# Cross-attention with LayerNorm: the order of the last stores, of the last products and of one tile's scaling

## The chip, the cores and the metric

The kernel runs on one core of one Trainium2 chip. The metric is the device time of one execution in microseconds (us). Times of the kernel before come from three runs and from one execution taken by the hardware profiler.

## What is computed

For each of 4 sequences, 2048 rows of 512 values attend to 77 context rows, with 16 heads of 32 columns. The result goes through an output projection, the input is added, and each row is normalised.

```
qs = x @ wq;  ks = ctx @ wk;  vs = ctx @ wv           # split in 16 heads of 32
scores = qs @ ks.T / sqrt(32);  scores[mask] = -inf
attn = softmax(scores) @ vs                            # heads joined again: 512 columns
out = attn @ wo + x
mu, var = mean(out), mean((out - mu)**2)               # over the 512 columns of a row
return (out - mu) / sqrt(var + 1e-5) * gamma + beta
```

## The kernel before

The 8192 rows are 64 tiles of 128 rows, two tiles to a block; tile 63 is the last. The order in which work is recorded is written out by hand: ORDER is a string of words, each a letter for a step and the number of a tile or block, and a loop runs through it. Each engine takes its instructions in this order and waits for others by semaphores. Buffers and PSUM banks are handed out by another table, SLOTS.

The words that matter here, for tile t:

- `Wt` is the product of the attention weights with the values (`av_tile`, TensorE). Before it, `U` words issue DMAs that regroup the transposed weights, each on the queue that its last letter names (s SyncE, a ScalarE, g GpSimd). `ct` and `dt` write the high part AH (ScalarE) and the low part AL (VectorE, L540) of that product.
- `Ot` is the output projection (`o_proj`, L579): for each of 4 chunks of 128 rows three products, AH with the high weights, AH with the low weights, AL with the high weights, all summed in one PSUM bank `po`. Some numbers in PADS put idle steps ahead of products.
- `+t`, `@t`, `$t`, `=t`, `st`, `ut` add the input and work out mean and inverse root: `$` adds into PSUM (VectorE, L591), `s` takes the statistics on VectorE (L630, L632), `=` takes them on ScalarE instead (L636, L637; tiles 60 and 62), `u` is the inverse root on GpSimd, two small operations (L645 or L643, then L646), and `@` is `u` and one step more.
- Two ways lead from there to the result. On one, `%t` scales and shifts on ScalarE (L654), and `ft` multiplies by gamma and adds beta on GpSimd (`affine`, L621 and L622). On the other, `yt` centres and multiplies by gamma on VectorE (L659), and `zt` multiplies by the inverse root and adds beta on VectorE (`finish`, L662). Tiles 52, 55, 58 and 61 end in `f`; tiles 54, 56, 57, 59, 60 and 62 end in `z`. Tile 63 ends in two halves, `>63.0` and `>63.1` (L666).
- `wt` stores the tile, always on SyncE's queue (`store`, L625). Tile 63's halves go out as `<63.0` on SyncE and `<63.1` on ScalarE (L672).

Rows of tiles 56 to 59 lie in a buffer called xth and those of tiles 60 to 63 in one called xtl; those before in buffers called o.

Of the kernel before, what the change touches and what calls it, by code (L numbers as in the profile page):

```python
# [13 lines left out]
ALU = mybir.AluOpType  # L14
# [15 lines left out]
NC_D = D // P  # L30
# [12 lines left out]
KSCALE = 1.0 / HD**0.5  # L43
LATE = 48
LAST = 56

# [89 lines left out]
m63.1 P30.7a b29.1 O58 %55 u57 t62 %53 f55 %52 $56 U62.2s U62.11a V30 $54 U62.1s U62.10a +58 U62.6s U62.3a f53 t63  # L138
U62.4a O59 a30.0 a30.1 s58 U63.4s U63.1a U63.11s b30.0 @58 U62.8a U62.9s b30.1 U62.0a s56 U62.7s O61 U63.9a U62.5g
y57 U63.10g U63.3a s54 U63.6g U63.0s U63.5a U63.7g U63.2s y54 U63.8a u54 w50 O60 +61 %58 f52 w53 z54 s61 $59 y56  # L140
W62 @61 s59 W63 c62 u56 z57 u59 c63 d62 O62 $60 f58 y59 =60 d63 z59 %61 y60 O63 w59 u60 =62 z56 w58 f61 z60 w57 y62
w56 w60 s63 w52 w55 u62 y63 w61 u63 z62 w54 w62 >63.0 <63.0 >63.1 <63.1
"""

SLOTS = {
# [33 lines left out]
def xattn_layernorm(  # L179
# [15 lines left out]
    nc = tc.nc  # L195
# [12 lines left out]
    def buf(shape, dtype, tag, name):  # L208
        pool = tiny if shape[-1] <= H else sb
        return pool.tile(shape, dtype, tag=tag + next(slots[tag]), name=name)  # L210

    def once(held, key, shape, dtype, tag):
        if key not in held:
            held[key] = buf(shape, dtype, tag, f"{tag}_{key}")
        return held[key]

    def bank(name):
        return ps.tile([P, 512], F32, tag="mm" + next(slots["mm"]), name=name)
# [6 lines left out]
    woh = const.tile([P, NC_D, D], F32R, name="woh")  # L225
    wol = const.tile([P, NC_D, D], F32R, name="wol")
    kct = const.tile([P, NG, NB, NK2], F32, name="kct")
    vsb = const.tile([NK2, NB, 2, D // 2], F32, name="vsb")
    gam = const.tile([P, D], F32, name="gam")
    bet = const.tile([P, D], F32, name="bet")  # L230
# [28 lines left out]
    od, pos, mvs, rns, vd, ris, parts = {}, {}, {}, {}, {}, {}, {}  # L259
# [17 lines left out]
    def pad_steps():  # L277
        n = int(next(pads, "0"), 36)
        return [0] + [n // 11 + (i < n % 11) for i in range(11)]

    def idle(n):
        for _ in range(n):
            nc.tensor.nop(hint="pad")
# [259 lines left out]
    def load_x(t):  # L543
        if t < LAST:
            od[t] = buf([P, D], F32, "o", name=f"o_{t}")
        else:
            od[t] = once(ends, t // 4, [P, 4, D], F32, "xth" if t < LAST + 4 else "xtl")[:, t % 4]
        nc.sync.dma_start(od[t], x[t * P : (t + 1) * P, :])
# [19 lines left out]
    def o_proj(t):  # L568
        b, tt = divmod(t, 2)
        rs = slice(tt * P, tt * P + P)  # L570
        ah, al = ahs[b], als[b]
        first = t not in pos
        if first:
            pos[t] = bank(f"po_{t}")
        steps = pad_steps()
        for c in range(NC_D):
            for n, (a, w) in enumerate(((ah, woh), (ah, wol), (al, woh))):
                idle(steps[3 * c + n])
                nc.tensor.matmul(  # L579
                    pos[t],  # L580
                    a[:, c, rs],
                    w[:, c, :],
                    start=(first and c == 0 and n == 0),
                    stop=(c == NC_D - 1 and n == 2),
                )

    def residual(t):
        nc.vector.tensor_tensor(od[t], pos.pop(t), od[t], ALU.add)
# [16 lines left out]
    def rsqrt(b):  # L605
        rn = rns[b] = buf([P, 2, 2], F32, "rn", name=f"rn_{b}")
        mv = mvs[b]
        nc.gpsimd.tensor_tensor(rn[:, 0, :], mv[:, :, 1], eps, ALU.add)
        nc.gpsimd.tensor_tensor(rn[:, 0, :], rn[:, 0, :], mhalf, ALU.pow)
        nc.gpsimd.tensor_tensor(rn[:, 1, :], mv[:, :, 0], rn[:, 0, :], ALU.mult)  # L610
        nc.gpsimd.tensor_tensor(rn[:, 1, :], rn[:, 1, :], mneg, ALU.mult)

    def scale(t):
        o = od[t]
        tt = t % 2
        rn = rns[t // 2]
        nc.scalar.activation(o, o, AF.Identity, bias=rn[:, 1, tt : tt + 1], scale=rn[:, 0, tt : tt + 1])

    def affine(t):
        o = od[t]  # L620
        nc.gpsimd.tensor_tensor(o, o, gam, ALU.mult)  # L621
        nc.gpsimd.tensor_tensor(o, o, bet, ALU.add)  # L622

    def store(t):
        nc.sync.dma_start(out[t * P : (t + 1) * P, :], od.pop(t))  # L625
# [14 lines left out]
    def rsqrt_one(t):  # L640
        mv = mvs[t, 1]
        if t in by_act:
            nc.gpsimd.tensor_scalar(mv[:, 2:3], mv[:, 1:2], 1.0 / D, EPS, ALU.mult, ALU.add)  # L643
        else:
            nc.gpsimd.tensor_tensor(mv[:, 2:3], mv[:, 1:2], eps[:, :1], ALU.add)  # L645
        nc.gpsimd.tensor_tensor(mv[:, 2:3], mv[:, 2:3], mhalf[:, :1], ALU.pow)  # L646
# [9 lines left out]
    def centre(t):  # L656
        o = pos.get(t, od[t])
        m, op = (3, ALU.add) if t in by_act else (0, ALU.subtract)
        nc.vector.scalar_tensor_tensor(o, o, mvs[t, 1][:, m : m + 1], gam, op, ALU.mult)  # L659

    def finish(t):
        nc.vector.scalar_tensor_tensor(od[t], pos.pop(t, od[t]), mvs[t, 1][:, 2:3], bet, ALU.mult, ALU.add)  # L662
# [23 lines left out]
    first = [buf([P, 2, BLK + D], F32, tag, name=f"first_{tag}") for tag in ("xtl", "xth")]  # L686
    first = [first[c // 2][:, c % 2] for c in range(NC_D)]
# [21 lines left out]
    for c in range(NC_D):  # L709
# [12 lines left out]
        for n, (w, r) in enumerate(((wqh, x0h), (wqh, x0l), (wql, x0h))):  # L722
            for m in range(NG):
# [4 lines left out]
                    start=(c == 0 and n == 0),  # L728
                    stop=(c == NC_D - 1 and n == 2),
# [13 lines left out]
    for c in range(0, NC_D, 2):  # L743
# [19 lines left out]
        "V": lambda k, part: av(k), "W": lambda k, part: av_tile(k), "a": av_hi, "b": av_lo,  # L763
        "c": lambda k, part: av_hi(k // 2, k % 2, True), "d": lambda k, part: av_lo(k // 2, k % 2, True),
        "x": lambda k, part: load_x(k), "X": lambda k, part: resid(k), "O": lambda k, part: o_proj(k),
        "+": lambda k, part: residual(k), "s": lambda k, part: (moments_one if k >= LATE else moments)(k),
        "v": lambda k, part: rsqrt(k), "k": lambda k, part: scale(k), "f": lambda k, part: affine(k),
        "u": lambda k, part: rsqrt_one(k), "y": lambda k, part: centre(k), "z": lambda k, part: finish(k),
        "w": lambda k, part: store(k), "*": lambda k, part: hold(k), "#": lambda k, part: residual_late(k),
        "&": lambda k, part: split_hi(k, nc.scalar), "~": lambda k, part: split_lo(k),  # L770
# [63 lines left out]
```

## Time and profile before

| What | Value |
|---|---|
| Runs | 509.96, 510.60, 510.66 us; median 510.6 |
| Span of the profiled execution | 508.1 us, first to last instruction |
| Busy in that span | TensorE 98%, VectorE 93%, ScalarE 92%, GpSimd 83% |
| SyncE's last DMA issues | from 498.40 to 504.70 us |
| ScalarE's last DMA issue | 505.10 us |

The span is that of one profiled execution. The page gives no other time of that execution, and the time of a run is some 2 us longer than the span. Times inside the span are counted from its first instruction. A row of a timeline gives start, length, engine and line, then what is written and read. Matmuls overlap, so a row's length is more than the distance to the next one.

### The profile page before, as it was taken

To read this page: it belongs to the slowest core of one execution; us is meant where nothing else is said; L and a number is where in the kernel's file an instruction comes from. 1 tells how busy PE (TensorE), PEld (TensorE's weight loads), DVE (VectorE), ACT (ScalarE), POOL (GpSimd) and SP (SyncE) were. 2 spreads that over 40 slices of the span, in tenths; PEclk is the share of its full clock that TensorE was granted. 3 is DMA by queue.
4 is the path that set the end of the run, shared out by engine and by line. 5 is a ranking of instruction groups with operands and counts; after the bars stand their busy time and mean duration, and the time that the engine had idled before them with its cause. 6 is when DMAs were issued, how large, how long until landed. Compare 5 with 4: busy or idle time off the path is not lost.

```text
span 508.1 us, 21810 instructions
## 1 busy us (share of the span) xinstructions
PE 497.6 (98%) x6834; PEld 384.0 (76%) x6834; DVE 471.3 (93%) x2565; ACT 465.6 (92%) x2228; POOL 420.0 (83%) x388
## 2 busy tenths in 40 slices
PE   8999999999999999999999999999999999999994
PEld 6987777777777777777777877777787777776663
DVE  5798999999999999999999999999999999999986
ACT  6699999998999999999999999999999999999622
POOL 2573756999978998989899898888989679999986
PEclk9999999999999999999999999999999999999999
DMA  8947767878987687796877678777777687777755
GB/s 298 397 154 215 177 185 171 239 195 237 261 239 220 192 243 198 204 261 189 237 205 239 198 218 229 213 226 211 225 207 219 182 225 214 209 210 198 213 153 228
DMA packets 59236, 110.96 MB, mean 218 GB/s; under 512 B 9430, under 2 KB 12270, under 8 KB 59126
## 3 DMA queue, kind: packets, MB, share of 16 engines
q1 hardware_dynamic: 54854, 101.63, 69.1%
q0 software_dynamic: 2624, 6.16, 4.4%
q10 hardware_dynamic: 1648, 1.77, 1.4%
q8 instruction: 60, 0.98, 0.9%
q14 instruction: 50, 0.41, 0.3%
HBM read 41.79 MB, written 16.78 MB: 115 GB/s over the span
## 4 chain that ended last, share of the span: by engine, by line
PE 85%; DVE 5%; DMA 4%; POOL 3%; SPq 2%; issue 1%; ACTq 0%; ACT 0%; DVEq 0%
PE pq L290 33%; PE po L579 28%; PE sc L414 10%; PE pa L507 10%; PE pv L341 2%; DVE pbuf L431 1%; DVE B L482 1%; PE pk L313 1%; DMA xtl<-x 1%; DMA PT<-B 1%; SPq L493 1%; DMA first_xth<-xw 1%; POOL mvt L646 1%; PE pq L724 1%; DVE q L304 0%
## 5 line engine op out<-in xcount | busy, mean ns | idle before, releaser
L446 ACT ACTIVATE pbuf<-pbuf,nm 128x77 f32<-128x77 f32 x1024 | 352.4, 350 | 3.6 <-DVE nm L431 3.4
L446 ACT ACTIVATION_READ_ACCUMULATOR pbuf<-pbuf,nm 128x1 f32 x1024 | 195.3, 191 | 0.0
L431 DVE CUSTOM_DVE_ANT_0 pbuf<-sc,mb 128x77 f32<-128x77 f32 x1024 | 170.8, 232 | 6.8 <-PE sc L414 3.6
L461 POOL TENSOR_TENSOR pbuf<-pbuf,ri 128x1232 f32<-128x1232 f32 x63 | 142.8, 2268 | 29.1 <-DVE ri L456 27.6
L579 PE MATMUL po<-woh,AH 128*128 128x512 f32 x256 | 102.1, 399 | 0.4 <-DVE nm L431 0.4
L290 PE MATMUL pq<-xth,wqh 128*128 128x512 f32 (+1 forms) x256 | 101.2, 395 | 0.3
L579 PE MATMUL po<-woh,AL 128*128 128x512 f32 x256 | 99.8, 390 | 0.8 <-DVE AL L540 0.8
L579 PE MATMUL po<-wol,AH 128*128 128x512 f32 x256 | 99.7, 390 | 0.0
L290 PE MATMUL pq<-xth,wql 128*128 128x512 f32 (+1 forms) x256 | 98.1, 383 | 0.0
L290 PE MATMUL pq<-xtl,wqh 128*128 128x512 f32 (+1 forms) x256 | 98.1, 383 | 0.0
L482 DVE STREAM_TRANSPOSE B<-pbuf 128x1280 f32<-128x1280 f32 x64 | 96.1, 1501 | 0.9 <-POOL pbuf L461 0.2
L431 DVE DVE_READ_ACCUMULATOR2_ANT nm<- 128x1 f32 x1024 | 83.8, 82 | 0.0
L273 POOL TENSOR_TENSOR xtl<-xtf,xth 128x1024 fp32r<-128x1024 f32 x28 | 67.3, 2406 | 4.3 <-ACT xth L269 4.3
L622 POOL TENSOR_TENSOR o<-o,bet 128x512 f32<-128x512 f32 x51 | 66.0, 1294 | 4.0
L414 PEld LDWEIGHTS sc<-kct,q 32*64 32x64 f32 x4096 | 51.2, 130 | 22.2 <-issue 11.0
L621 POOL TENSOR_TENSOR o<-o,gam 128x512 f32<-128x512 f32 x51 | 67.0, 1314 | 0.2 <-issue 0.2
L414 PE MATMUL sc<-kct,q 32*64 32x77 f32 x4096 | 60.6, 238 | 0.0
L507 PE MATMUL pa<-PT,vsb 96*32 96x256 f32 x992 | 59.7, 382 | 0.0
L579 PEld LDWEIGHTS po<-woh,AH 128*128 128x128 f32 x256 | 48.0, 188 | 13.9 <-issue 1.7
L290 PEld LDWEIGHTS pq<-xth,wqh 128*128 128x128 f32 x256 | 48.1, 188 | 12.3 <-issue 1.2
L579 PEld LDWEIGHTS po<-woh,AL 128*128 128x128 f32 x256 | 48.1, 188 | 11.6 <-DVE AL L540 1.5
L290 PEld LDWEIGHTS pq<-xth,wql 128*128 128x128 f32 x256 | 48.1, 188 | 9.7
(127 smaller groups left out, 641.9 us busy)
## 6 DMA issues: line engine op xcount, KB each, us to landing
PT<-B SPq DMA_DIRECT2D x337, 128.0 KB
xtf<-xT SPq DMA_DIRECT2D x28, 512.0 KB
o<-x SPq DMA_DIRECT2D x56, 256.0 KB
out<-o SPq DMA_DIRECT2D x56, 256.0 KB
PT<-B POOLq DMA_DIRECT2D x29, 128.0 KB, 3.9
stage_a<-wk SPq DMA_DIRECT2D x4, 256.0 KB
stage_b<-wo SPq DMA_DIRECT2D x4, 256.0 KB
stage_a<-xT SPq DMA_DIRECT2D x2, 512.0 KB
```

The source lines that it names most:

```text
L273: nc.gpsimd.tensor_tensor(l[:, c : c + 2], fx.pop((g, c)), xh[g][:, c : c + 2].bitcast(F32), ALU.subtract)
L290: nc.tensor.matmul(pq, w[:, c, m * P : (m + 1) * P], r[g][:, c, rs], start=(n == 0), stop=(n == 11))
L341: nc.tensor.matmul(pv[: rows.stop - rows.start], ctx_s[c][i][:, rows], v[c], start=(n == 0), stop=(n == 11))
L414: mm = nc.tensor.matmul(sc[j][r0 : r0 + SR, g * NK : (g + 1) * NK], qs[q, g, rs.start + r0 : rs.start + r0 + SR], kct[q, g, t // TPB, keys ...
L431: nc.vector.tensor_tensor_reduce(pb[:, h // 2, (h % 2) * NK : (h % 2 + 1) * NK], scs[t][j][:, g * NK : (g + 1) * NK], mb[:, t % TPB, keys_ ...
L446: nc.scalar.activation(pb[:, h // 2, (h % 2) * NK : (h % 2 + 1) * NK], pb[:, h // 2, (h % 2) * NK : (h % 2 + 1) * NK], AF.Exp, bias=nmax[t ...
L461: nc.gpsimd.tensor_tensor(pv, pv, rv.to_broadcast((P, NP, 2, NK)), ALU.mult)
L482: nc.vector.transpose(bt.rearrange("p c q r -> p q c r"), pbuf[t % NPB].rearrange("p q (c r) -> p q c r", c=5),)
L507: nc.tensor.matmul(pas[b, g // 2][HD * j : HD * (j + 1), (g % 2) * BLK : (g % 2 + 1) * BLK], vsb[:, 2 * b // TPB, h % 2, HD * (h // 2) : H ...
L579: nc.tensor.matmul(pos[t], a[:, c, rs], w[:, c, :], start=(first and c == 0 and n == 0), stop=(c == NC_D - 1 and n == 2),)
L621: nc.gpsimd.tensor_tensor(o, o, gam, ALU.mult)
L622: nc.gpsimd.tensor_tensor(o, o, bet, ALU.add)
```

## The change

Three edits at the end of the program. The stores of tiles 55, 54, 52 and 57 are recorded before that of tile 59. The projections of tiles 62 and 63 take their eight products with AH first and the four with AL last. Tile 61's `f` is split in its two operations, written `|61.0` and `|61.1`: the multiplication now stands behind the inverse root of tile 62, the addition behind that of tile 63, and with that tile 62's `z` moves ahead of tile 63's statistics, and tile 61's store to the end.

```diff
+LOW_LAST = 62
...
-W62 @61 s59 W63 c62 u56 z57 u59 c63 d62 O62 $60 f58 y59 =60 d63 z59 %61 y60 O63 w59 u60 =62 z56 w58 f61 z60 w57 y62
-w56 w60 s63 w52 w55 u62 y63 w61 u63 z62 w54 w62 >63.0 <63.0 >63.1 <63.1
+W62 w55 w54 @61 s59 W63 c62 w52 u56 z57 u59 c63 d62 O62 $60 w57 f58 y59 =60 d63 z59 %61 y60 O63 w59 u60 =62 z56 w58
+z60 w56 u62 y62 w60 |61.0 z62 s63 w62 u63 y63 |61.1 >63.0 <63.0 >63.1 <63.1 w61
...
-        for c in range(NC_D):
-            for n, (a, w) in enumerate(((ah, woh), (ah, wol), (al, woh))):
-                idle(steps[3 * c + n])
...
+        terms = [(c, a, w) for c in range(NC_D) for a, w in ((ah, woh), (ah, wol), (al, woh))]
+        if t >= LOW_LAST:
+            terms.sort(key=lambda term: term[1] is al)
+        for i, (c, a, w) in enumerate(terms):
+            idle(steps[i])
+            nc.tensor.matmul(pos[t], a[:, c, rs], w[:, c, :], start=(first and i == 0), stop=(i == len(terms) - 1))
...
     def affine(t):
-        o = od[t]
-        nc.gpsimd.tensor_tensor(o, o, gam, ALU.mult)
-        nc.gpsimd.tensor_tensor(o, o, bet, ALU.add)
+        affine_step(t, 0)
+        affine_step(t, 1)
+
+    def affine_step(t, i):
+        nc.gpsimd.tensor_tensor(od[t], od[t], (gam, bet)[i], (ALU.mult, ALU.add)[i])
```

GpSimd (POOL), its last rows before. In a name the number after the letters is the tile; mvt holds a tile's statistics, gam and bet are gamma and beta, and xtl is here tile 61.

```order
L643 TENSOR_SCALAR mvt_60_10505<-mvt_60_10505 128x1
L646 TENSOR_TENSOR mvt_60_10505<-mvt_60_10505,small_78 128x1
L621 TENSOR_TENSOR xtl_15_8749<-xtl_15_8749,gam_76 128x512
L622 TENSOR_TENSOR xtl_15_8749<-xtl_15_8749,bet_77 128x512
L643 TENSOR_SCALAR mvt_62_10527<-mvt_62_10527 128x1
L646 TENSOR_TENSOR mvt_62_10527<-mvt_62_10527,small_78 128x1
L645 TENSOR_TENSOR mvt_63_10541<-mvt_63_10541,small_78 128x1
L646 TENSOR_TENSOR mvt_63_10541<-mvt_63_10541,small_78 128x1
```

The same place on GpSimd after the change:

```order
L642 TENSOR_SCALAR mvt_60_10509<-mvt_60_10509 128x1
L645 TENSOR_TENSOR mvt_60_10509<-mvt_60_10509,small_78 128x1
L642 TENSOR_SCALAR mvt_62_10531<-mvt_62_10531 128x1
L645 TENSOR_TENSOR mvt_62_10531<-mvt_62_10531,small_78 128x1
L621 TENSOR_TENSOR xtl_15_8749<-xtl_15_8749,gam_76 128x512
L644 TENSOR_TENSOR mvt_63_10546<-mvt_63_10546,small_78 128x1
L645 TENSOR_TENSOR mvt_63_10546<-mvt_63_10546,small_78 128x1
L621 TENSOR_TENSOR xtl_15_8749<-xtl_15_8749,bet_77 128x512
```

Tile 61's two operations stood together ahead of the roots of 62 and 63; now one stands between these roots and one behind both.

VectorE (DVE), its last rows before; po is a tile's PSUM bank, and the outputs called xtl are rows of tiles 60, 62 and 63 in turn.

```order
L662 SCALAR_TENSOR_TENSOR xtl_15_8749<-po_60_10413,mvt_60_10505,bet_77 128x512
L659 SCALAR_TENSOR_TENSOR po_62_10208<-po_62_10208,mvt_62_10527,gam_76 128x512
L630 BN_STATS st_63_10539<-po_63_10153 128x6
L632 BN_AGGR mvt_63_10541<-st_63_10539 128x2
L659 SCALAR_TENSOR_TENSOR po_63_10153<-po_63_10153,mvt_63_10541,gam_76 128x512
L662 SCALAR_TENSOR_TENSOR xtl_15_8749<-po_62_10208,mvt_62_10527,bet_77 128x512
L666 SCALAR_TENSOR_TENSOR xtl_15_8749<-po_63_10153,mvt_63_10541,bet_77 128x256 x2
```

The same place on VectorE after the change:

```order
L661 SCALAR_TENSOR_TENSOR xtl_15_8749<-po_60_10413,mvt_60_10509,bet_77 128x512
L658 SCALAR_TENSOR_TENSOR po_62_10208<-po_62_10208,mvt_62_10531,gam_76 128x512
L661 SCALAR_TENSOR_TENSOR xtl_15_8749<-po_62_10208,mvt_62_10531,bet_77 128x512
L629 BN_STATS st_63_10544<-po_63_10153 128x6
L631 BN_AGGR mvt_63_10546<-st_63_10544 128x2
L658 SCALAR_TENSOR_TENSOR po_63_10153<-po_63_10153,mvt_63_10546,gam_76 128x512
L665 SCALAR_TENSOR_TENSOR xtl_15_8749<-po_63_10153,mvt_63_10546,bet_77 128x256 x2
```

Tile 62's last operation moved from behind tile 63's statistics and centring to ahead of them.

SyncE (SP), its last rows before; these are stores but for the first row, which regroups weights, and the four rows of xth are tiles 59, 58, 57 and 56.

```order
L493 DMA PT_31_10313<-B_31_10306 32x2x256 x9
L625 DMA out<-o_50_9983 128x512
L625 DMA out<-o_53_9503 128x512
L625 DMA out<-xth_14_9206 128x512 x4
L625 DMA out<-xtl_15_8749 128x512
L625 DMA out<-o_52_9350 128x512
L625 DMA out<-o_55_9797 128x512
L625 DMA out<-xtl_15_8749 128x512
L625 DMA out<-o_54_10119 128x512
L625 DMA out<-xtl_15_8749 128x512
L672 DMA out<-xtl_15_8749 128x256
```

SyncE after the change; the four rows of xth are now tiles 57, 59, 58 and 56, and the rows of xtl tiles 60 and 62, the half of 63, and 61.

```order
L494 DMA PT_31_10313<-B_31_10306 32x2x256 x9
L624 DMA out<-o_50_9983 128x512
L624 DMA out<-o_53_9503 128x512
L624 DMA out<-o_55_9797 128x512
L624 DMA out<-o_54_10119 128x512
L624 DMA out<-o_52_9350 128x512
L624 DMA out<-xth_14_9206 128x512 x4
L624 DMA out<-xtl_15_8749 128x512 x2
L671 DMA out<-xtl_15_8749 128x256
L624 DMA out<-xtl_15_8749 128x512
```

The stores of tiles 55, 54 and 52 went ahead of the four of xth, and tile 61's whole store from before tile 54's to behind the first half of tile 63.

More of the change, by code (lines that the diff above doesn't have):

```diff
@@ L575, in o_proj @@
         steps = pad_steps()
-        for c in range(NC_D):
-            for n, (a, w) in enumerate(((ah, woh), (ah, wol), (al, woh))):
-                idle(steps[3 * c + n])
[L579 to L585, printed above, removed]
+        terms = [(c, a, w) for c in range(NC_D) for a, w in ((ah, woh), (ah, wol), (al, woh))]
[4 more added lines that the diff above has]
+            nc.tensor.matmul(pos[t], a[:, c, rs], w[:, c, :], start=(first and i == 0), stop=(i == len(terms) - 1))
     def residual(t):
@@ L766, in xattn_layernorm @@
         "+": lambda k, part: residual(k), "s": lambda k, part: (moments_one if k >= LATE else moments)(k),
-        "v": lambda k, part: rsqrt(k), "k": lambda k, part: scale(k), "f": lambda k, part: affine(k),
+        "v": lambda k, part: rsqrt(k), "k": lambda k, part: scale(k), "f": lambda k, part: affine(k), "|": affine_step,
         "u": lambda k, part: rsqrt_one(k), "y": lambda k, part: centre(k), "z": lambda k, part: finish(k),
```

## The prediction

> **What bounds the kernel now.** I read the page first. Then I went to the end of the program, since only that is edited.
>
> ```profile
> span 508.1 us, 21810 instructions
> ```
>
> The first rows that the change moves stand, in time, after the last score work; up to about 488 us both programs are the same on every engine. So the question is what sets the time from 488 us to 508.1 us. The page gives no time of the profiled execution beside its span; the three runs (509.96 to 510.66) are 1.9 to 2.6 us above it. I work out a difference against the span and put it on the median, 510.6.
>
> Second view: SyncE's own rows and what its queue waited for (start, length, then the DMA issued).
>
> ```profile
> SPq L625 <- DVE xth L662: 9.5, 1, 9.5
> ...
> 487.70 1.09 SPq L625 DMA_DIRECT2D out<-o  x2
> 498.40 1.88 SPq L625 DMA_DIRECT2D out<-xth  x4
> ...
> 504.18 0.33 SPq L625 DMA_DIRECT2D out<-xtl  x1
> 504.70 0.33 SPq L672 DMA_DIRECT2D out<-xtl  x1
> ```
>
> The queue stands for 9.5 us at the store of tile 59, while stores that are ready lie behind it. What was kept back goes out between 498.40 and 504.70, where the last row is the first half of tile 63. Third view, the DMA share by stretches (the last two columns are the DMA share and GB/s):
>
> ```profile
> 495.00:499.00 4.00, 3.22 (x15) 2.55 (x14) 4.00 (x8) 2.59 (x7) 3.78 (x5) 1.00 0.00 0
> 499.00:499.20 0.20, 0.20 (x2) 0.19 (x1) 0.20 (x2) 0.20 (x2) 0.17 (x1) 1.00 0.00 0
> 499.20:500.00 0.80, 0.80 (x5) 0.66 (x4) 0.61 (x2) 0.77 (x3) 0.72 (x3) 1.00 0.97 376
> 500.00:501.00 1.00, 1.00 (x6) 0.66 (x4) 1.00 (x2) 0.10 (x2) 1.00 (x1) 1.00 1.04 404
> 506.40:506.60 0.20, 0.00 (x0) 0.00 (x0) 0.00 (x0) 0.00 (x0) 0.00 (x0) 0.50 0.21 62
> ```
>
> Nothing moves until 499.2, then the DMA engines are full until about 506.5, at some 404 GB/s: a 256 KB store takes 262144 B / 404 GB/s = 0.65 us. So a backlog of stores does reach into the tail. But it hides little. The last one is the second half of tile 63, which ScalarE issues when VectorE has computed it:
>
> ```profile
> 503.40 0.75 DVE L662 SCALAR_TENSOR_TENSOR xtl<-po,mvt,bet 128x512 f32<-128x512 f32 x1 [0.46 <-POOL mvt L646]
> 504.19 0.87 DVE L666 SCALAR_TENSOR_TENSOR xtl<-po,mvt,bet 128x256 f32<-128x256 f32 x2
> 505.10 0.36 ACTq L672 DMA_DIRECT2D out<-xtl  x1
> ```
>
> SyncE's first store went out at 498.40 and its bytes moved from 499.2: 0.8 us from issue to first byte. A half store alone (0.33 us) issued at 505.10 would therefore have landed by 505.10 + 0.8 + 0.33 = 506.2; it landed by about 506.5. The backlog costs the end 0.3 us, and behind the last byte come 1.6 us to the span's end, which the change does not touch.
>
> **The change part by part.** *Stores.* Tiles 55, 54, 52 and 57 go ahead of 59. Their results are ready early:
>
> ```profile
> 482.27 1.28 POOL L622 TENSOR_TENSOR o<-o,bet 128x512 f32<-128x512 f32 x1
> 491.01 0.75 DVE L662 SCALAR_TENSOR_TENSOR o<-po,mvt,bet 128x512 f32<-128x512 f32 x1 [1.07 <-POOL mvt L646]
> 492.31 1.27 POOL L622 TENSOR_TENSOR o<-o,bet 128x512 f32<-128x512 f32 x1
> 494.55 0.72 DVE L662 SCALAR_TENSOR_TENSOR xth<-po,mvt,bet 128x512 f32<-128x512 f32 x1
> ```
>
> These are the last operations of 55, 54, 52 and 57, so the issues fall at about 488.8, 491.8, 493.6 and 495.3, and 4 x 0.65 = 2.6 us of transfers leave the full stretch. What is left from 498.40 on is bound by when results come, not by bytes. The backlog term is 0.3 us, and it is all that this edit can give. What it may cost: the store of 55 now shares the DMA engines with the last regrouping transfers of tile 63. They are over by 492.8 (the DMA share behind it is nil), and the value product of tile 63 starts at 493.40, after a wait on another releaser:
>
> ```profile
> 492.80:493.20 0.40, 0.14 (x8) 0.00 (x0) 0.40 (x2) 0.14 (x1) 0.40 (x1) 1.00 0.00 0
> 493.40 1.08 PE L522 MATMUL pa<-PT,vsb 96*32 96x128 f32 x32 [0.47 <-DVE po L591]
> ```
>
> One more store delays them by at most 0.65 us, to 493.4: no loss there, and if there is one, the next part shows that TensorE has slack. Nothing but stores stands behind the moved ones on SyncE.
>
> *The low part last.* Tile 62's third product now waits for AL; products with it come ninth to twelfth after the change.
>
> ```profile
> 494.75 0.40 PE L579 MATMUL po<-wol,AH 128*128 128x512 f32 x1
> 495.92 0.50 PE L579 MATMUL po<-woh,AL 128*128 128x512 f32 x1 [0.78 <-DVE AL L540]
> 496.26 0.40 PE L579 MATMUL po<-woh,AH 128*128 128x512 f32 x1
> 496.49 0.39 PE L579 MATMUL po<-wol,AH 128*128 128x512 f32 x1
> 500.81 0.39 PE L579 MATMUL po<-woh,AL 128*128 128x512 f32 x1
> ```
>
> Products are 0.23 us apart, so without the wait the third starts near 494.98 and everything behind it comes 0.94 earlier; TensorE ends at 501.20 - 0.94 = 500.26. The ninth would start near 496.36, when the low part is written (the first of the two rows below ends at 495.87; the second, tile 63's, ends at 497.72, and is wanted near 499.2).
>
> ```profile
> 495.19 0.68 DVE L540 TENSOR_TENSOR AL<-pa,AH 128x512 fp32r<-128x512 f32 x1
> 497.04 0.68 DVE L540 TENSOR_TENSOR AL<-pa,AH 128x512 fp32r<-128x512 f32 x1
> ```
>
> On the path this is worth nothing by itself: VectorE takes up tile 63's statistics only when it gets there, and ScalarE is behind its own work when tile 62's projection ends. If this edit fails to pull TensorE forward, its end at 501.20 is still before the 501.88 worked out next.
>
> *Tile 61's end.* This is the edit on the path. VectorE and GpSimd from 499 us:
>
> ```profile
> 499.89 0.75 DVE L662 SCALAR_TENSOR_TENSOR xtl<-po,mvt,bet 128x512 f32<-128x512 f32 x1 [0.19 <-POOL mvt L646]
> 500.56 0.75 DVE L659 SCALAR_TENSOR_TENSOR po<-po,mvt,gam 128x512 f32<-128x512 f32 x1
> 501.24 0.70 DVE L630 BATCH_NORM_STATS2 st<-po 128x6 f32<-128x512 f32 x1
> 501.97 0.18 DVE L632 BATCH_NORM_AGGREGATE mvt<-st 128x2 f32<-128x6 f32 x1
> 502.19 0.76 DVE L659 SCALAR_TENSOR_TENSOR po<-po,mvt,gam 128x512 f32<-128x512 f32 x1
> ...
> 499.82 1.29 POOL L621 TENSOR_TENSOR xtl<-xtl,gam 128x512 f32<-128x512 f32 x1
> 501.19 1.26 POOL L622 TENSOR_TENSOR xtl<-xtl,bet 128x512 f32<-128x512 f32 x1
> 502.54 0.20 POOL L643 TENSOR_SCALAR mvt<-mvt 128x1 f32<-128x1 f32 x1
> 502.82 0.55 POOL L646 TENSOR_TENSOR mvt<-mvt,small 128x1 f32<-128x1 f32 x1
> 503.60 0.55 POOL L646 TENSOR_TENSOR mvt<-mvt,small 128x1 f32<-128x1 f32 x1
> ...
> 499.91 0.19 ACT L637 ACTIVATION_READ_ACCUMULATOR xtl<-po,mvt 128x1 f32 x1
> ```
>
> Before, tile 61's multiply and add (499.82 to 502.45) stand ahead of both inverse roots, and VectorE waits 0.46 us for tile 62's. After, on GpSimd: tile 62's root follows ScalarE's sum (500.10), 500.15 to 500.97 (0.82 for its two steps, 502.54 to 503.37 before); then the multiply to 502.25. On VectorE: tile 62's finish goes from 501.22 to 501.9, with its root there by 500.97; tile 63's statistics start at 501.88 and end 0.91 later (as 501.24 to 502.15 before), at 502.79; centring runs 502.83 to 503.6. Tile 63's root starts at 502.82 and takes 0.82: 503.64. So the two halves of tile 63 start at 503.66 instead of 504.19: **0.53 us earlier**. ScalarE issues the second half at 505.10 - 0.53 = 504.57, and it lands near 504.57 + 0.8 + 0.33 = 505.7.
>
> But tile 61's add, which was over at 502.45, now comes after tile 63's root: 503.61 to 504.89, and its whole store is issued behind it, at 504.92, as the program's last. First byte 504.92 + 0.8 = 505.72, plus 0.65: 506.4. Against 506.5 before: **0.1 us** is left of the 0.53. The new last store is issued 0.18 us before the old one, but is twice as large. The sum: +0.53 for the two halves, -0.43 given back to tile 61, net -0.1 us: span 508.0, time 510.6 - 0.1 = **510.5 us**.
>
> The 0.8 us to first byte is the term I lean on. The Trainium skill, "DMA: Bandwidth & Descriptors", section "Specifications", gives about 0.6 us for this path and a limit of about 358 GB/s on memory for a core. The trace has 0.8 us (498.40 to 499.2) and 404 GB/s, so it does not agree, and the trace decides; by the page's figures the last store would land near 504.92 + 0.6 + 0.73 = 506.25, an estimate, and the time would be 510.3.
>
> **The rivals.** *Faster: tile 61's store is hidden.* If its add starts earlier than I place it, or its store overlaps the half stores with no delay of its own, tile 63's halves set the end and the whole 0.53 us stays: 510.1 us. For it speaks that the DMA engines are empty then; against it that the add must come after tile 63's root in GpSimd's order, and 256 KB need 0.65 us. Chance 0.17, of which 0.09 is over 0.2% (1.0 us, about what a measurement of this kernel can tell from no change): for that the time must fall below 509.6, which also takes a pace before that was in truth nearer to the lowest run, 509.96.
>
> *Slower: GpSimd's own end.* The end of the program has drains on each engine:
>
> ```profile
> L830 POOLq DRAIN  x3: 46/102/3783, 503.6 to 507.9; - x3
> L830 SPq DRAIN  x3: 7/7/7, 507.3 to 507.6; - x3
> ```
>
> GpSimd's first drain starts at 503.6 and takes 3.78 us, to about 507.4, though its last operation ended at 504.15. Either it only stood until SyncE's drains (507.3), or it needs 3.2 us after the last operation whatever SyncE does. In the second case moving GpSimd's last operation from 504.15 to 504.89 moves the end by 0.74: 511.3 us. It decides as soon as 3.2 us behind GpSimd's last operation is later than SyncE's last wait, which in these rows lie within 0.1 us of each other. For over 0.2% GpSimd would have to end at 505.2, 0.3 us later than I place it, as when tile 63's statistics slip. Against it: SyncE's row explains the same time without it. Chance 0.18, of which 0.1 is over 0.2%.
>
> *Not what it says:* if the store of 55 held up tile 63's transfers by more than its 0.65 us, TensorE's 0.94 us and VectorE's arrival at 501.88 leave 1.6 us of slack, so the time would stay at 510.5. Chance 0.05, in the forecast's class.
>
> **How the numbers follow.** The forecast as worked out has 0.6; with the milder parts of the rivals, within 0.2% holds 0.81, faster 0.09, slower 0.10. The range takes in the faster rival, 510.1, less about 0.4 us for a median that may sit nearer to the lowest run, and the slower one, 511.3: 509.7 to 511.4.
>
> **What would show it.** In the changed kernel's profile: SyncE has no 9.5 us wait with ready stores behind it; the DMA share is below full between 499 and 504; VectorE's wait of 0.46 for tile 62's root is gone and tile 63's halves start near 503.66; GpSimd's last row is tile 61's add, ending near 504.9, and SyncE's last issue follows it. I am wrong if the last bytes move after 506.6 or before 506.0, if statistics of tile 63 start later than 502, or if GpSimd's drain again ends 3.2 us after its last operation and later than SyncE's.

## The result and the profile after

The change made the kernel slower: 511.61 us (median of 9 runs, 511.07 to 512.5) against 510.6 us (9 runs, 509.85 to 511.2). The ratio is 1.0024, with an interval of 1.0016 to 1.0033. The forecast was 510.5 us in a range of 509.7 to 511.4, in effect no change. The rival that came true is the one called GpSimd's own end, and a second cause of the same size, the way of the last store to the end, had been taken to need no longer than before.

The span of the profiled execution went from 508.1 to 510.3 us. Not all of that is the change. The last transposition of attention weights (tile 63's) on VectorE stands ahead of everything that the change moves; its rows in the two timelines, before and after:

```profile
482.32 1.50 DVE L482 STREAM_TRANSPOSE B<-pbuf 128x1280 f32<-128x1280 f32 x1
```

```profile
483.46 1.50 DVE L483 STREAM_TRANSPOSE B<-pbuf 128x1280 f32<-128x1280 f32 x1
```

That execution was already 1.14 us late there, in code that both kernels share. From this row to the end it is 25.8 us before and 26.8 after: 1.0 us more, which is what the runs say. I compare times from this row on.

SyncE's issues after the change, and what its queue waited for:

```profile
489.03 5.96 SPq L624 DMA_DIRECT2D out<-o  x5
496.34 4.76 SPq L624 DMA_DIRECT2D out<-xth  x4
501.71 1.85 SPq L624 DMA_DIRECT2D out<-xtl  x2
505.46 0.33 SPq L671 DMA_DIRECT2D out<-xtl  x1
506.17 0.33 SPq L624 DMA_DIRECT2D out<-xtl  x1
```

```profile
SPq L624 <- DVE xth L661: 4.3, 3, 2.7
SPq L829 <- DMA out<-xtl: 2.3, 3, 1.4
```

The wait of 9.5 us at tile 59 is gone and the stores go out as they become ready. The last issue is now tile 61's whole store. The DMA share by stretches (last two columns) shows that the backlog has gone too:

```profile
503.00:504.00 1.00, 0.00 (x0) 0.00 (x0) 0.96 (x3) 0.00 (x0) 0.28 (x1) 1.00 0.23 86
505.00:506.00 1.00, 0.00 (x0) 0.00 (x0) 0.82 (x2) 0.00 (x0) 1.00 (x1) 1.00 0.00 0
507.10:507.80 0.70, 0.00 (x0) 0.00 (x0) 0.00 (x0) 0.00 (x0) 0.00 (x0) 0.50 1.05 392
507.80:508.20 0.40, 0.00 (x0) 0.00 (x0) 0.00 (x0) 0.00 (x0) 0.00 (x0) 0.50 0.07 26
508.20:508.40 0.20, 0.00 (x0) 0.00 (x0) 0.00 (x0) 0.00 (x0) 0.00 (x0) 0.50 0.03 10
```

In 505 to 506 nothing moves, where before all engines were full:

```profile
505.00:506.00 1.00, 0.00 (x0) 0.00 (x0) 0.06 (x1) 0.00 (x0) 0.00 (x0) 0.89 1.04 388
```

Yet the last bytes come as late as 508.3.

VectorE and GpSimd in the same stretch:

```profile
500.93 0.75 DVE L661 SCALAR_TENSOR_TENSOR xtl<-po,mvt,bet 128x512 f32<-128x512 f32 x1 [0.20 <-POOL mvt L645]
501.60 0.75 DVE L658 SCALAR_TENSOR_TENSOR po<-po,mvt,gam 128x512 f32<-128x512 f32 x1
502.45 0.75 DVE L661 SCALAR_TENSOR_TENSOR xtl<-po,mvt,bet 128x512 f32<-128x512 f32 x1
503.12 0.69 DVE L629 BATCH_NORM_STATS2 st<-po 128x6 f32<-128x512 f32 x1
504.06 0.76 DVE L658 SCALAR_TENSOR_TENSOR po<-po,mvt,gam 128x512 f32<-128x512 f32 x1
504.95 0.87 DVE L665 SCALAR_TENSOR_TENSOR xtl<-po,mvt,bet 128x256 f32<-128x256 f32 x2
...
504.37 0.55 POOL L645 TENSOR_TENSOR mvt<-mvt,small 128x1 f32<-128x1 f32 x1
504.88 1.26 POOL L621 TENSOR_TENSOR xtl<-xtl,bet 128x512 f32<-128x512 f32 x1
```

Tile 63's halves start 21.49 us behind the transposition, against 21.87 before (504.19 - 482.32): 0.38 earlier. GpSimd's last row is tile 61's addition, ending at 506.14; from the transposition that is 22.68, against 21.83 before: 0.85 later.

The drains at the end, after the change (start of the first and of the last one; lengths in ns, least, middle and longest):

```profile
L829 POOLq DRAIN  x3: 46/102/5012, 504.3 to 510.0; - x3
L829 SPq DRAIN  x3: 7/7/7, 509.4 to 509.8; - x3
```

GpSimd's long drain starts at 504.3 and ends 5.01 us later, at 509.3: 3.2 us behind its last operation, as before. SyncE gets to its drains at 509.4. So two ends run side by side. Counted from the transposition, GpSimd's came 0.85 us later and SyncE's about 1.0 us later (507.3 - 482.32 = 25.0 us behind it before, 509.4 - 483.46 = 25.9 after).

### The profile page after: what moved, and what is told of

Its sections match the earlier page's. It is cut to its first block, busy times and chain, and to the rows that moved or that the text cites. A ratio compares the mean times of both kernels' runs of the same rounds, so it can differ in the third digit from the quotient of the medians.

```text
span 510.3 us, 21814 instructions
## 1 busy us (share of the span) xinstructions
PE 498.4 (98%) x6834; PEld 384.9 (75%) x6834; DVE 471.2 (92%) x2565; ACT 465.9 (91%) x2228; POOL 419.7 (82%) x388
## 4 chain that ended last, share of the span: by engine, by line
PE 81%; DVE 10%; POOL 4%; DMA 2%; issue 1%; SPq 1%; ACT 0%; POOLq 0%; DVEq 0%
PE pq L291 32%; PE po L582 26%; PE sc L415 10%; PE pa L508 9%; DVE pbuf L432 3%; DVE B L483 3%; PE pv L342 2%; PE pk L314 1%; POOL PT L494 1%; DMA PT<-B 1%; DMA first_xtl<-xw 1%; PE pq L723 1%; POOL pbuf L462 1%; DVE st L629 1%; POOL mvt L645 1%
## 5 line engine op out<-in xcount | busy, mean ns | idle before, releaser
L415 PEld LDWEIGHTS sc<-kct,q 32*64 32x64 f32 x4096 | 51.8, 130 | 22.4 <-issue 11.1
L415 PE MATMUL sc<-kct,q 32*64 32x77 f32 x4096 | 61.1, 238 | 0.1
L291 PEld LDWEIGHTS pq<-xth,wqh 128*128 128x128 f32 x256 | 48.1, 188 | 12.4 <-issue 1.2
```

Of the source, the lines that this page charges most:

```text
L291: nc.tensor.matmul(pq, w[:, c, m * P : (m + 1) * P], r[g][:, c, rs], start=(n == 0), stop=(n == 11))
L415: mm = nc.tensor.matmul(sc[j][r0 : r0 + SR, g * NK : (g + 1) * NK], qs[q, g, rs.start + r0 : rs.start + r0 + SR], kct[q, g, t // TPB, keys ...
```

## The experiments

Ratios are to the kernel before, run beside each; 0.1% is 0.5 us. Theory A says that the last store's landing costs the time, theory B that GpSimd's drain does, theory C that the early stores do.

**The early stores alone (e1).** The words of tile 61, and the products, as before:

```diff
-W62 @61 s59 W63 c62 u56 ...
+W62 w55 w54 @61 s59 W63 c62 w52 u56 z57 u59 c63 d62 O62 $60 w57 f58 y59 =60 d63 z59 %61 y60 O63 w59 u60 =62 z56 w58 f61 z60 w56 y62
+w60 s63 u62 y63 w61 u63 z62 w62 >63.0 <63.0 >63.1 <63.1
```

> The kernel before with the early stores alone (tiles 55, 54, 52, 57 ahead of 59); tile 61 ends as before. Theory A, the last store: the 1 us is lost because tile 61's whole store is now the last one, issued late and slow to land; here it is not, the backlog is gone, so 0.3 us faster than before. Theory B, GpSimd's own end: its drain needs 3.2 us behind its last operation, and that is where it was, so no change (within 0.1 us). Theory C, the early stores hurt by sharing the DMA engines: about 1 us slower.

Measured 1.0006 (0.9993 to 1.0019): no change. Theory C's 1 us lies at the very end of the interval or outside, and so is a gain over 0.4 us. Its profile suggests why the backlog's 0.3 us did not come back, though it is one execution, and one that took 1.1 us more than before from the transposition to the end (26.9 against 25.8), which the medians of the runs (0.3 us apart) do not bear out. First its value product of tile 63, then VectorE:

```profile
495.03 1.08 PE L522 MATMUL pa<-PT,vsb 96*32 96x128 f32 x32 [1.50 <-DVE st L630]
...
502.21 0.76 DVE L659 SCALAR_TENSOR_TENSOR po<-po,mvt,gam 128x512 f32<-128x512 f32 x1 [1.15 <-ACT xtl L637]
503.45 0.70 DVE L630 BATCH_NORM_STATS2 st<-po 128x6 f32<-128x512 f32 x1 [0.48 <-PE po L579]
```

The product starts 12.2 us behind the transposition (whose row begins at 482.85 in e1), not 11.1 as before, and with the low part in the old order VectorE then waits 1.15 and 0.48 us for what follows from it.

**The low part last, alone (e2).** The last two lines of ORDER are those of before; what stays of the change is this:

```diff
+LOW_LAST = 62
...
+        if t >= LOW_LAST:
+            terms.sort(key=lambda term: term[1] is al)
```

> The kernel before with the products of the low part last for tiles 62 and 63 alone. All theories: no change within 0.2 us; TensorE's last product ends some 0.9 us earlier and nobody waits for it.

Measured 1.0010 (0.9994 to 1.0025): no change that can be told. TensorE's lead is used by nobody: in e2's profile tile 63's halves start 21.87 us behind the transposition, as before.

**The split alone (e3).** The stores of 52, 54 and 55 stay late, the products keep the old order (LOW_LAST = 64), and tile 61 ends as in the change:

```diff
+z60 w57 u62 y62 w56 w60 |61.0 z62 s63 w52 w55 w54 w62 u63 y63 |61.1 >63.0 <63.0 >63.1 <63.1 w61
```

> The kernel before with tile 61's split alone: its addition behind tile 63's root, tile 62's finish ahead of tile 63's statistics, its store last; the other stores stay late. Theory A: at least 1.0 us slower, more than the whole change if the backlog of stores is still there when the last is issued. Theory B: 1.0 us slower, like the whole change, whatever the stores do. Theory C: no slower than before.

Measured 1.0024 (1.0012 to 1.0037): the whole loss, from this part alone. A and B both said so.

**One more GpSimd operation (e4).** The kernel before, with an operation at GpSimd's end that feeds nothing:

```diff
+    def extra():
+        pb = pbuf[1][:, 0:4, 0:P]
+        nc.gpsimd.tensor_tensor(pb, pb, gam.rearrange("p (a b) -> p a b", a=4), ALU.mult)
...
-... u63 z62 w54 w62 >63.0
+... u63 !0 z62 w54 w62 >63.0
```

> The kernel before with one more GpSimd operation (128x512, on a buffer that nobody reads again) behind its last; it feeds nothing and no store waits for it. Theory A: no change within 0.2 us. Theory B: the operation's length, some 1.2 us, is added to the time. Theory C: no change.

Measured 1.0021 (1.0007 to 1.0034), 1.1 us slower, for an operation that no store and no engine waits for. Theory A alone is out. The drains of e4:

```profile
L834 POOLq EVENT_SEMAPHORE  x4: 17/17/17, 509.6 to 510.3; - x4
L834 POOLq DRAIN  x3: 46/102/5019, 504.6 to 510.1; - x3
L834 SPq DRAIN  x3: 7/7/7, 508.3 to 509.8; - x3
```

SyncE is at its drains at 508.3, but GpSimd's drain runs until 504.6 + 5.0 = 509.6, and only there does GpSimd go on. This is GpSimd's own end, alone.

**The dead addition (e5).** The changed kernel without the late store: it leaves tile 61's addition of beta out and stores tile 61 right behind its multiplication, and a like operation on a buffer that nobody reads stands in the addition's place.

```diff
-z60 w56 u62 y62 w60 |61.0 z62 s63 w62 u63 y63 |61.1 >63.0 <63.0 >63.1 <63.1 w61
+z60 w56 u62 y62 w60 |61.0 w61 z62 s63 w62 u63 y63 !0 >63.0 <63.0 >63.1 <63.1
```

> The changed kernel, but tile 61's addition of beta is left out: tile 61 is stored right behind its multiplication, and an operation of the same size on a buffer that nobody reads stands last on GpSimd in its place. So no late store, but GpSimd's late end. Theory A, the last store: the loss is gone, 0 to 0.4 us faster than before. Theory B, GpSimd's own end (drain 3.2 us behind its last operation): still 0.9 us slower than before.

Measured 1.0012 (0.9999 to 1.0025); the median is 0.87 us above before. The interval just touches no change, so the runs alone lean to B without settling it. Its profile has B's picture:

```profile
L833 POOLq DRAIN  x3: 46/102/5019, 504.9 to 510.4; - x3
L833 SPq DRAIN  x3: 7/7/7, 508.5 to 510.2; - x3
```

GpSimd's drain ends at 509.9, SyncE has been ready since 508.5.

**The addition first (e6).** The changed kernel with tile 61's addition ahead of tile 63's root, so that neither the late store nor GpSimd's late end is there.

```diff
+... |61.0 z62 |61.1 s63 w62 w61 u63 y63 >63.0 <63.0 >63.1 <63.1
```

> The changed kernel, but tile 61's addition stands ahead of tile 63's root, so that the root is GpSimd's last operation, 0.7 us earlier than in the changed kernel and 0.26 us later than before; tile 61's store is not the last. Theory A: within 0.1 us of before. Theory B: 0.2 to 0.3 us slower than before, 0.7 us faster than the changed kernel.

Measured 1.0004 (0.9993 to 1.0014): the loss is gone. With the early stores and the new product order still in, this shows that the place of the one addition, with the store behind it, is the cause.

**The last store alone (e7).** The kernel before, with only tile 61's store moved behind the first half of tile 63.

```diff
-... y63 w61 u63 z62 w54 w62 >63.0 <63.0 >63.1 <63.1
+... y63 u63 z62 w54 w62 >63.0 <63.0 >63.1 <63.1 w61
```

> The kernel before with tile 61's store moved behind the first half of tile 63 on SyncE's queue, and nothing else: GpSimd's work is as before. Theory A: 0.7 to 1.1 us slower. Theory B: no change to 0.3 us slower, since GpSimd's drain ends where it did and the last bytes come at most 0.3 us later.

Measured 1.0017 (1.0006 to 1.0028), 1.06 us in the medians: B alone is out too. A had it right. GpSimd ends as before, and SyncE is the later one:

```profile
505.33 0.41 SPq L625 DMA_DIRECT2D out<-xtl  x1
...
L830 POOLq DRAIN  x3: 46/102/3787, 503.8 to 508.9; - x3
L830 SPq DRAIN  x3: 7/7/7, 508.4 to 508.7; - x3
```

GpSimd's drain ends at 503.8 + 3.8 = 507.6; SyncE's comes at 508.4, 3.0 us behind the last issue at 505.33.

**The addition on VectorE (e8, e9).** Versions meant to be faster than before: tile 61's addition moves to VectorE, so that GpSimd ends early and no whole store is last. In e9 the store of 54 also goes ahead of 55, and tile 63's centring ahead of tile 62's finish.

```diff
+        eng = nc.vector if t == 61 and i else nc.gpsimd
+        eng.tensor_tensor(od[t], od[t], (gam, bet)[i], (ALU.mult, ALU.add)[i])
...
+z60 w56 |61.0 y62 w60 u62 s63 u63 |61.1 w61 z62 w62 y63 >63.0 <63.0 >63.1 <63.1     # e8
+z60 w56 |61.0 y62 w60 u62 s63 u63 |61.1 w61 y63 z62 w62 >63.0 <63.0 >63.1 <63.1     # e9
```

> The changed kernel with tile 61's multiplication ahead of tile 62's root on GpSimd and its addition on VectorE behind tile 63's statistics, so that GpSimd ends with tile 63's root, some 1.1 us earlier than before, and no whole store is last. Both theories: 0.3 to 0.4 us faster than before, bound then by tile 63's halves; theory B alone says that GpSimd's drain is over 0.8 us before SyncE's last wait.

> Kernel e8 with the store of tile 54 ahead of that of 55 on SyncE, so that 55 waits for tile 54's end and leaves the DMA engines to tile 63's regrouping, and with tile 63's centring ahead of tile 62's finish on VectorE. From the rows of the runs so far: tile 63's value product starts some 6.3 us before tile 60's finish, as before, not 5.1; tile 63's halves start 4.15 us behind it (4.30 before, 4.63 in e8); GpSimd's drain is not the later end. Both theories together: 0.2 to 0.4 us faster than before. If the early stores' sharing does not matter (theory C wrong): the same as e8.

Measured 0.9997 (0.9985 to 1.001) and 1.0001 (0.9987 to 1.0015): no difference from before that can be told, and a gain of 0.2 to 0.4 us can neither be seen nor ruled out. In e8's profile the halves start 22.13 us behind the transposition, later than the 21.87 of before, so the gain that I expected there had lost its ground. No version is shown to beat the kernel before. In e9's profile the product of tile 63 and the halves are where I put them:

```profile
483.44 1.50 DVE L483 STREAM_TRANSPOSE B<-pbuf 128x1280 f32<-128x1280 f32 x1
494.65 1.08 PE L523 MATMUL pa<-PT,vsb 96*32 96x128 f32 x32 [0.50 <-DVE po L588]
500.97 0.75 DVE L662 SCALAR_TENSOR_TENSOR xtl<-po,mvt,bet 128x512 f32<-128x512 f32 x1 [0.17 <-POOL mvt L646]
505.01 0.87 DVE L666 SCALAR_TENSOR_TENSOR xtl<-po,mvt,bet 128x256 f32<-128x256 f32 x2
```

The product starts 11.2 us behind the transposition and 6.3 ahead of tile 60's finish, the halves 4.04 behind that finish (4.30 before).

**54 ahead of 55 in the changed kernel (e10).**

```diff
-W62 w55 w54 @61 s59 W63 c62 w52 u56 ...
+W62 w54 w55 @61 s59 W63 c62 w52 u56 ...
```

> The changed kernel with the store of tile 54 ahead of that of 55 on SyncE and nothing else. If the store of 55 was what held tile 63's regrouping up, the value product of tile 63 starts about 6.3 us before tile 60's finish instead of 5.5. The time, by theories A and B, stays 0.9 to 1.0 us above before, since both late ends are untouched; by theory C it comes back to before.

Measured 1.0021 (1.0005 to 1.0038): A and B again, not C. In its profile TensorE was late already from further up, and both value products ran without a gap, so it does not show the distance that I wanted to read.

## Why the prediction was wrong

Two steps of the prediction failed. It held that the 1.6 us from the last byte to the end are not touched by the change and that GpSimd's drain only waits for SyncE; the runs show that this drain ends 3.20 us behind GpSimd's last operation and can itself set the end (e4). And it priced tile 61's store, as the last one, at 0.8 + 0.65 us and kept the time behind its landing as it was; with nothing but that store moved to the end (e7), SyncE's drains came about 0.9 us later, though the last issue stood 22.8 us behind the transposition as before.

The time of the profiled executions fits one rule: the span ends about 0.8 us behind the later of two ends, SyncE's drains, which come when the last store has landed and been waited for, and GpSimd's drain, 3.2 us behind its last operation. From the profiles:

| Kernel | GpSimd's last operation ends | its drain ends | SyncE's first drain | span | time, ratio |
|---|---|---|---|---|---|
| before | 504.2 | 507.4 | 507.3 | 508.1 | 1 |
| after | 506.1 | 509.3 | 509.4 | 510.3 | 1.0024 |
| e4, GpSimd late alone | 506.4 | 509.6 | 508.3 | 510.4 | 1.0021 |
| e7, store last alone | 504.4 | 507.6 | 508.4 | 509.2 | 1.0017 |
| e6, neither | 504.5 | 507.7 | 507.6 | 508.5 | 1.0004 |

Before, the two ends lie within 0.1 us. The change moved each by about a microsecond, so either alone costs nearly the whole loss, and the two do not add up. Which of them is last in the changed kernel is a matter of tenths: SyncE's by 0.1 us in its one profile and by 0.3 in e3's, GpSimd's by 0.5 in e10's.

*The drain: a wrong choice between two readings.* The prediction shows the row, and I gave the reading "it only stood until SyncE's drains" the better chance. In all twelve profiles the drain ends 3.20 us behind GpSimd's last operation, whether SyncE comes before (e4) or after it (e7). The Trainium skill, "VectorE: DVE Perf Modes", section "The DRAIN you can't avoid", calls the drains at a program's start and end boilerplate of about 12 ns on all five engines; SyncE's rows of 7 ns are near that, GpSimd's 3.2 us are not, and the measurement decides. The rival's mechanism was right, and its price of 0.74 us was close: GpSimd ended 0.85 us later.

*The last store: a term that was mis-sized.* I priced the way from issue to landing at 0.8 + 0.65 us, the same 1.45 us as before, and left the way from landing to the end alone. From the last issue to SyncE's first drain it took 507.3 - 505.1 = 2.2 us before, and 509.4 - 506.17 = 3.2 after. Where the last one is a half store it took 2.1 to 2.3 us in all eight profiles of that kind, and where it is tile 61's whole store 2.7 to 3.5 in four (after, e3, e7, e10). Split at the last packet of the last store, it is about 1.4 + 0.7 us before and 2.1 + 1.1 after (1.8 to 2.6 and 0.8 to 0.9 in e3, e7 and e10), so both the priced way to landing and the way behind it grew. A part of it is plain: ScalarE's half, issued just ahead, moves its bytes first. The queues in two stretches after the last issue:

```profile
q10 hardware_dynamic: 104, 0.11, 101.2%
...
q1 hardware_dynamic: 133, 0.26, 96.9%
q10 hardware_dynamic: 32, 0.02, 7.9%
```

From 506.8 to 507.1 only ScalarE's queue (q10) moves, and tile 61's bytes (q1) fill 507.1 to 507.8. Behind them a few packets straggle until 508.3, and the queue list of 507.8 to 508.2 has an instruction fetch among them:

```profile
q14 instruction: 1, 0.01, 4.8%
q1 hardware_dynamic: 9, 0.00, 2.4%
```

That the fetch holds up the last packet is only what single executions suggest: in e3's profile a fetch from 506.7 to 507.0 stands ahead of the store's last eight packets in the same way, while in e7 and e10 it comes behind the last one, and e7 lost as much in the runs. What makes up the rest stays open. The Trainium skill, "DMA: Bandwidth & Descriptors", section "Anatomy of one DMA — SWDGE (gpsimd) path", has a fixed cost of about 2.0 us and the bytes at 436 GB/s, fitted to DMAs issued from GpSimd: an estimate of 2.3 us for a half store and 2.6 for a whole one. The half stores here, issued from ScalarE and counted to SyncE's drain, come near it (2.1 to 2.3), the whole ones took longer (2.7 to 3.5).

*Tile 63's halves: 0.38 of 0.53 us.* I took 0.67 us, the distance between independent VectorE operations, for tile 62's finish too. It now stands right behind its own centring, whose result it reads, and starts 502.45 - 501.60 = 0.85 us behind it, 0.10 after that one's end. In e8 the halves start as far behind tile 63's centring:

```profile
504.43 0.75 DVE L659 SCALAR_TENSOR_TENSOR po<-po,mvt,gam 128x512 f32<-128x512 f32 x1
505.28 0.88 DVE L666 SCALAR_TENSOR_TENSOR xtl<-po,mvt,bet 128x256 f32<-128x256 f32 x2
```

In the changed kernel itself they start 0.89 us behind the centring, but there it is tile 63's root that they follow, as I had it: the root ends at 504.37 + 0.55 = 504.92, and they start at 504.95.

*The store of 55 and tile 63.* I allowed 0.65 us of delay to the value product. It starts 11.6 to 12.4 us behind the transposition in after, e1, e5, e6 and e8, where 55 goes first, 0.5 to 1.3 more than the 11.1 of before; it is 11.0 to 11.4 in e2, e3, e4 and e7, and 11.2 in e9. Each is one execution. I had also read the product's row as a wait on another releaser than the transfers, but the operation it names had been over for 0.24 us when the product started at 493.40:

```profile
492.49 0.67 DVE L591 TENSOR_TENSOR po<-po,xth 128x512 f32<-128x512 f32 x1
```

So that row did not show that the regrouped weights had come in time. The slack that I named covered the delay in the changed kernel, and the delay of 0.9 us there used up the 0.94 that the new product order gains: TensorE ends 18.8 us behind the transposition (501.18 + 1.07 - 483.46), against 18.9 before. That the new product order is what covers it rests on e1's one profile, where VectorE waits without it.

What came as forecast: the wait of 9.5 us and the backlog went, TensorE's lead is worth nothing by itself (e2), and GpSimd's last row is tile 61's addition with the last issue behind it.

## What to carry to other kernels

Read the end of a program as several ends side by side: the last store until it has been waited for, and each engine's last operation with its drain. Work that nobody waits for still has to end somewhere; here it should not be GpSimd's last, since 3.2 us follow it. And in this program a small store belongs last. Where two ends are equal, making either one later costs time (e4, e7); by the same rule making only one of them earlier should gain nothing, which no run here tried by itself.

## What the runs showed of the hardware

GpSimd's closing drain took 3.20 us beyond its last operation in each of twelve profiles. VectorE's and ScalarE's first drains in the kernel before lasted under 1 us:

```profile
L830 DVEq DRAIN  x2: 19/465/911, 504.2 to 507.6; - x2
L830 ACTq DRAIN  x2: 8/70/133, 505.8 to 507.6; - x2
```

VectorE's ends at 505.1, just behind its last operation (504.19 + 0.87). Two 128x512 operations on VectorE of which the second reads the first one's result started 0.85 us apart (tile 62's centring and finish after the change), independent ones 0.67. And ahead of the first edited instruction, in code that all kernels share, profiled executions lay up to 1.7 us apart (the transposition at 482.2 to 484.0 in eleven of the twelve; in e10, with TensorE late, at 484.6), so two spans are not to be compared without a common row.
